# DIN recommendation layer: the loop over the history, laid out by four groups of 32 partitions

## The chip, the core and the metric

The kernel runs on one core of a Trainium2 chip. The metric is the device time of one execution in microseconds (us). The kernel before takes 36928.09 us, the median of 3 runs (36926.46 to 36942.14). A separate execution under the hardware profiler gives the profile; its own time was 36762.96 us, of which the program's span (first to last instruction) is 36760.7 us.

## The reference

A batch of 16384 users, each with a history of 200 items; all tables have rows of d = 64 float32 values. Cut to what matters:

```
h    = i_emb[hist]                                  # (200, 16384, 64): a gather
feat = concat([h, it, h - it, h * it])              # it: the candidate item, the same for all 200
a    = dice(feat @ au_W1 + au_b1, au_alpha, axis=1) # 36 hidden units; moments over the batch
w    = a @ au_W2 + au_b2                            # one weight for each (history place, user)
cur  = sum(w * h, axis=0)                           # (16384, 64)
z    = concat([u_emb[user], it, c_emb[cate], cur])
z    = dice(z @ W1 + b1, alpha1, axis=0); z = dice(z @ W2 + b2, alpha2, axis=0)
out  = z @ W3 + b3

dice(x, alpha): p = sigmoid((x - mean) / sqrt(var + 1e-8)); x * (p + alpha * (1 - p))
```

The moments of the first dice are those of one history place over the whole batch, so a place's gates can be worked out only when all 16384 users of that place have gone through the first layer.

## The kernel before

**The table.** Since `feat @ au_W1` is linear in `h` but for the product term, a first stage builds in DRAM a `table` with 128 values for each of the 100000 items: the row `h` (64 values) and `h @ (W_h + W_diff)` (36 values, padded). It also forms `xi`, the share of the candidate item with the bias, `itT`, the candidate rows turned, and `ucT`, the rows of user and category turned for the last layers. In this first stage each block of the table goes through `transpose` (L223), a matmul (L240) and `transpose_back` (L231).

**The loop.** The batch is cut into ND = 8 parts of 2048 users: TD = 16 tiles of 128 rows each. The loop runs over 200 places times 8 parts, so over 1600 steps, plus ten steps that only drain. A hardware loop (`For_i`) holds 24 places (192 steps) and runs 7 times; the last 32 places and the drain are written out. The order of the work on each engine is the order in the code (`manual_schedule`). One `step(k)` works on four parts at once:

- `fetch(k)`: 16 indirect DMAs from GpSimd (POOL, L202), each of 128 table rows of 512 bytes, into `land[k % 12]`, and one plain DMA of `xi` from SyncE (SP, L369) into `xit[k % 2]`.
- the gates of part k-10, on ScalarE (ACT): sigmoid of x (L452), then a scale and an offset per hidden unit (L455), into the PSUM tile `pg`.
- `turn(k-1)`: both halves of the gathered rows are turned so that d, or the hidden unit, lies on partitions. VectorE (DVE) transposes blocks of 32 x 32. Four instructions over 64 partitions each (L377), because a turned part has the 64 values of d on two groups of 32 partitions and two sets of rows beside them. ACT copies the turned rows into PSUM (`ph`, L458).
- `hidden(k-2)`: x = `px` + the turned table part (L390), written over the table half of `land`, and the batch statistics (L392).
- ACT copies `xit` into `px` (L462), and `product(k-1)`: `hm` = rows times candidate (L384), then `blk_m` times `hm` onto `px` on TensorE (PE, L240).
- `weights(k-10)`: gates times x (L398), a transposition back over 128 partitions (L400), a sum over 32 values (L402).
- `weigh(k-10)`: the two partial sums of a row lie on different partitions, so 64 partitions are moved (`r1`, L410) and added with the bias into PSUM (`w`, two instructions of 64 partitions, L413); then w times the rows (L418) and the sum onto `cur` (L419).
- every eighth step, `moments`: the statistics of two groups of partitions are joined by four copies of 32 partitions (L429) and a chain of small DVE instructions (L431 to L254), with a square root on ACT (L249).

`land` has 12 buffers, and step k-2 is the last to read the buffer that `fetch(k)` writes. Most DVE instructions of the loop take one operand from PSUM and one from SBUF. After the loop come two dense layers and the output.

Of the kernel before, what the change touches and what calls it, by code (L numbers as in the profile page):

```python
# [28 lines left out]
def din_kernel(  # L29
# [50 lines left out]

    parts = [(0, S), (S, A - S)]

# [3 lines left out]
    blk_h = once.tile([P, P], F32, name="blk_h")  # L86
    blk_i = once.tile([P, P], F32, name="blk_i")
    blk_m = const.tile([P, P], F32, name="blk_m")
    au_w = once.tile([P, 4, A], F32, name="au_w")
    au_bias = const.tile([P, 1], F32, name="au_bias")  # L90
    au_al = const.tile([P, 1], F32, name="au_al")
    au_1al = const.tile([P, 1], F32, name="au_1al")
    au_w2 = const.tile([P, 1], F32, name="au_w2")
# [4 lines left out]
    for e in range(2):  # L98
        rows = au_W1.rearrange("(g d) a -> d g a", d=D)[e * S : (e + 1) * S]
        for g in range(2):  # L100
            r = quarter(e, g)
            nc.sync.dma_start(au_w[r], rows)
            for q, (a0, n) in enumerate(parts):
                c, a = quarter(q, g, n), slice(a0, a0 + n)
                nc.vector.tensor_add(blk_h[r, c], au_w[r, 0, a], au_w[r, 2, a])
                nc.vector.tensor_sub(blk_i[r, c], au_w[r, 1, a], au_w[r, 2, a])
                nc.vector.tensor_copy(blk_m[r, c], au_w[r, 3, a])
    for g in range(2):
        for q, (a0, n) in enumerate(parts):
            r, a = quarter(q, g, n), slice(a0, a0 + n)  # L110
            nc.sync.dma_start(au_bias[r], col(au_b1)[a])
            nc.sync.dma_start(au_al[r], col(au_alpha)[a])
            nc.sync.dma_start(au_w2[r], au_W2[a])
# [11 lines left out]
    idx = [const.tile([P, NT], I32, name=f"idx{i}") for i in range(IDX)]  # L125
    stats = [const.tile([P, 2 * ND, nc.vector.BN_STATS_DIM], F32, name=f"st{i}") for i in range(2)]
    rstds = [const.tile([P, 1], F32, name=f"rs{i}") for i in range(2)]
    shifts = [const.tile([P, 1], F32, name=f"sh{i}") for i in range(2)]
    px, pz = (psum.tile([P, CD], F32, name=n) for n in ("px", "pz"))
# [6 lines left out]
    ucT = dram.tile([2, ND, P, CD], F32, name="ucT")  # L136
# [18 lines left out]
        n: const.tile([n * m, n * m], F32, name=f"mean{n}") for n, m in ((ZA, 2), (ZB, 2 * J), (Z2, 2))  # L155
# [53 lines left out]
    def load_ids(t, ids):  # L209
        nc.sync.dma_start(t, ids.rearrange("(p n) -> p n", n=NT))  # L210

# [3 lines left out]
    def by_tile(t, i):  # L215

        return t[:, ts(i, CH)].rearrange("p (n t) -> p n t", t=S)

    def transpose(dst, rows, n=TD):

        for i in range(2):
            for e in range(2):
                nc.vector.transpose(  # L223
                    by_tile(dst[ts(e, D)], i)[:, :n], rows[ts(i, D), :n, ts(e, S)]
                )

    def transpose_back(rows, src, n=TD):

        for i in range(2):
            for e in range(2):  # L230
                nc.vector.transpose(  # L231
                    rows[ts(i, D), :n, ts(e, S)], by_tile(src[ts(e, D)], i)[:, :n]
                )

    def layer(dst, pairs, n=CH, onto=False):

        for i in range(2):
            cols = slice(i * CH, i * CH + n)
            for j, (lhsT, rhs) in enumerate(pairs):
                nc.tensor.matmul(  # L240
                    dst[:, cols], lhsT, rhs[:, cols],
                    start=(j == 0 and not onto), stop=(j == len(pairs) - 1),
                    skip_group_check=onto,
                )
# [13 lines left out]
    ids = [once.tile([P, NT], I32, name=f"ids{i}") for i in range(3)]  # L258
    for t, v in zip(ids, (r_item, r_user, r_cate)):
        load_ids(t, v)  # L260
# [11 lines left out]
    def table_rows(b):  # L272
# [11 lines left out]
        transpose(rT, tab, m)  # L284
        layer((px, pz)[b % 2], [(blk_h, rT)], n=m * S)
        tabs[b] = tab, m

    def table_store(b):
        n0, n = blocks[b]
        tab, m = tabs.pop(b)  # L290
        transpose_back(tab[:, :, D:], (px, pz)[b % 2], m)
# [9 lines left out]
    def keep_one(j):  # L301
        c, k = j % ND, j // ND
        if k == 0:
            transpose(itT[:, c], land[j % EARLY])
            layer(ph, [(blk_i, itT[:, c])])
            t = pre.tile([P, CD], F32, tag="t", name="t")
            nc.scalar.activation(t, ph, AF.Identity, bias=au_bias)
            nc.scalar.dma_start(xi[c], t)
        else:
            t = pre.tile([P, CD], F32, tag="t", name="t")  # L310
            transpose(t, land[j % EARLY])
            nc.scalar.dma_start(ucT[k - 1, c], t)
# [22 lines left out]
    with ExitStack() as main:  # L335
# [15 lines left out]
        layer(px, [(blk_m, hx[0][:, 0])])  # L351
        nc.vector.bn_stats(stats[-1 % 2][:, 0, :], hx[0][:, 0, :CH])
        for c in range(1, 2 * ND):
            nc.vector.tensor_copy(stats[-1 % 2][:, c, :], stats[-1 % 2][:, 0, :])
# [16 lines left out]
        def turn(k):  # L371

            rows = land[k % LAND].rearrange("p n (s e c) -> p n s e c", s=2, e=2)
            for i in range(2):
                for e in range(2):
                    dst = hx[k % 2][ts(e, D), :, ts(i, CH)]
                    nc.vector.transpose(  # L377
# [293 lines left out]
```

## Time and profile before

| | |
|---|---|
| median of 3 runs | 36928.09 us |
| profiled execution | 36762.96 us |
| its span | 36760.7 us |
| POOL, first loop gather to last | 590.45 to 36527.96 us of the span |
| DVE busy | 25445.5 us (69%) |
| POOL busy | 24516.5 us (67%) |
| ACT busy | 7755.0 us (21%) |
| PE busy | 6368.2 us (17%), mean granted clock 0.542 |
| DMA | 73 GB/s on average |

In a row of the groups stand the line, the engine, the operation, what it writes and reads, the shapes and how often; then the busy time in us and the mean of one in ns; then the time for which the engine was idle just before such instructions, and what ended it. "issue" means that the engine waited for nothing that the profile shows.

### The profile page before, as it was taken

Reading aid. Unit: us, or ns where it says so; the run is one execution under the profiler, and the core shown is the slowest. Engines: PE = TensorE matmul, PEld = TensorE weight load, DVE = VectorE, ACT = ScalarE, POOL = GpSimd, SP = SyncE. Lnnn points to the kernel's source line nnn. Section 1 sums busy time; section 2 is a strip of 40 time slices with the busy share of each in tenths; the row PEclk is TensorE's granted clock in tenths of the full one; section 3 lists DMA queues with packets and bytes.
Section 4 is the critical chain, followed back from the end, with each engine's and each line's share of the span. In section 5 each row is a group of like instructions: output and inputs, shape, how many; then the busy total and the mean of one; then the engine's idle time right before and its main releaser. Section 6 shows DMA issues by size and latency. Waiting matters only on the chain. (4 is left out here: it accounts for less than half of the span.)

```text
span 36760.7 us, 100656 instructions
## 1 busy us (share of the span) xinstructions
PE 6368.2 (17%) x7006; PEld 2037.9 (6%) x7006; DVE 25445.5 (69%) x28797; ACT 7755.0 (21%) x7105; POOL 24516.5 (67%) x25991
## 2 busy tenths in 40 slices
PE   2111111111111111111111111111111111221112
PEld 0000000000000000000000000000000000000000
DVE  6767666676667666676667666676767666676767
ACT  0222222222222222222222222222222222222222
POOL 6666666666666666666666666666666666666665
PEclk5555555555555555555555555555555555555555
DMA  4222222222222222222222222222222222222222
GB/s 138 71 71 71 70 70 70 72 71 70 70 71 71 70 70 70 72 70 70 70 71 71 70 71 69 71 71 70 71 70 71 70 71 74 80 79 73 71 71 59
DMA packets 1214773, 2667.86 MB, mean 73 GB/s; under 512 B 551244, under 2 KB 577388, under 8 KB 1207916
## 3 DMA queue, kind: packets, MB, share of 16 engines
q0 software_dynamic: 831488, 1691.97, 17.5%
q1 hardware_dynamic: 372012, 906.09, 8.1%
q10 hardware_dynamic: 10560, 63.79, 0.4%
q14 instruction: 692, 5.67, 0.1%
q8 instruction: 21, 0.34, 0.0%
HBM read 2590.90 MB, written 69.16 MB: 72 GB/s over the span
## 5 line engine op out<-in xcount | busy, mean ns | idle before, releaser
L202 POOL DMA_INDIRECT land<-table,idx x25600 | 24153.1, 943 | 11825.8 <-issue 11629.5
L240 PE MATMUL px<-hx,blk_m 128*128 128x512 f32 x6408 | 5929.4, 1080 | 29931.8 <-DVE hx L384 15789.1
L377 DVE STREAM_TRANSPOSE hx<-land 64x1024 f32<-64x1024 f32 x6404 | 7920.8, 1237 | 2071.6 <-issue 1973.1
L452 ACT ACTIVATE pg<-land,sh,rs 128x1024 f32<-128x1024 f32 x1610 | 1943.8, 1207 | 18443.1 <-DVE cur L419 12618.3
L240 PEld LDWEIGHTS px<-hx,blk_m 128*128 128x128 f32 x6408 | 1880.8, 324 | 33947.3 <-issue 33947.3
L413 DVE SCALAR_TENSOR_TENSOR ph<-r,au_bias,r 64x16 f32<-64x16 f32 x3220 | 775.5, 241 | 3084.0 <-issue 2883.1
L458 ACT COPY ph<-hx 128x1024 f32<-128x1024 f32 x1601 | 1627.6, 1017 | 5996.1 <-DVE hx L377 3240.6
L418 DVE TENSOR_TENSOR pg<-land,ph 128x1024 f32<-128x1024 f32 x1610 | 1978.4, 1229 | 1190.7 <-issue 1158.6
L402 DVE TENSOR_REDUCE r<-hx 128x32 f32<-128x1024 f32 x1610 | 1964.1, 1220 | 584.2 <-issue 342.4
L400 DVE STREAM_TRANSPOSE hx<-pg 128x1024 f32<-128x1024 f32 x1610 | 2012.8, 1250 | 233.1 <-DVE pg L398 133.3
L392 DVE BATCH_NORM_STATS2 st<-land 128x6 f32<-128x512 f32 x3204 | 2061.2, 685 | 55.1
L390 DVE TENSOR_TENSOR land<-px,hx 128x1024 f32<-128x1024 f32 x1602 | 1962.1, 1225 | 69.7 <-issue 21.2
L419 DVE TENSOR_TENSOR cur<-pg,cur 128x1024 f32<-128x1024 f32 x1610 | 1970.9, 1224 | 55.6
L398 DVE TENSOR_TENSOR pg<-pg,land 128x1024 f32<-128x1024 f32 x1610 | 1957.3, 1216 | 2.7 <-ACT pg L455 2.5
L384 DVE TENSOR_TENSOR hx<-ph,itT 128x1024 f32<-128x1024 f32 x1601 | 1945.2, 1215 | 0.0
L455 ACT ACTIVATE pg<-pg,au_al,au_1al 128x1024 f32<-128x1024 f32 x1610 | 1895.0, 1177 | 54.4
L462 ACT COPY px<-xit 128x1024 f32<-128x1024 f32 x1601 | 1627.2, 1016 | 403.3 <-issue 257.6
L410 DVE COPY r<-r 64x32 f32<-64x32 f32 x1610 | 370.7, 230 | 1194.5 <-issue 976.6
L429 DVE COPY other<-mv 32x2 f32<-32x2 f32 x804 | 139.0, 173 | 1134.5 <-issue 1133.8
L249 ACT ACTIVATE std<-var,eps 128x1 f32<-128x1 f32 x201 | 59.2, 294 | 3361.8 <-DVE var L439 2823.8
L452 ACT ACT_TABLE_LOAD x209 | 268.1, 1283 | 394.1 <-DMA table<-tab 320.0
L439 DVE SCALAR_TENSOR_TENSOR var<-dev,half 128x1 f32<-128x1 f32 x201 | 44.2, 220 | 437.1 <-remote 411.2
(122 smaller groups left out, 2101.9 us busy)
## 6 DMA issues: line engine op xcount, KB each, us to landing
xit<-xi SPq DMA_DIRECT2D x1601, 512.0 KB
land<-table,idx POOLq DMA_INDIRECT x25600
table<-tab ACTq DMA_DIRECT2D x48, 1024.0 KB
tab<-in_L_rec_i_emb SPq DMA_DIRECT2D x48, 512.0 KB
zt<-ucT SPq DMA_DIRECT2D x32, 512.0 KB
idx<-in_r_hist SPq DMA_DIRECT2D x200, 64.0 KB
ucT<-t ACTq DMA_DIRECT2D x16, 512.0 KB
zbase<-zt SPq DMA_DIRECT2D x10, 512.0 KB
```

The source lines that it names most:

```text
L202: nc.gpsimd.indirect_dma_start(out=dst[:, n, :], out_offset=None, in_=rows, in_offset=bass.IndirectOffsetOnAxis(ap=ids[:, n : n + 1], axis=0),
L240: nc.tensor.matmul(dst[:, cols], lhsT, rhs[:, cols], start=(j == 0 and not onto), stop=(j == len(pairs) - 1), skip_group_check=onto,)
L377: nc.vector.transpose(dst.rearrange("p s (n t) -> p n s t", t=S), rows[ts(i, D), :, :, e])
L384: nc.vector.tensor_mul(hm, ph, itT[:, k % ND])
L390: nc.vector.tensor_add(x_of(k), by_row(px), by_row(hx[k % 2][:, 1]))
L392: nc.vector.bn_stats(stats[l % 2][:, 2 * c + i, :], x_of(k)[:, ts(i, TD // 2)])
L398: nc.vector.tensor_mul(by_row(pg), by_row(pg), x_of(k))
L400: nc.vector.transpose(yT, pg)
L402: nc.vector.tensor_reduce(r, yT.rearrange("p (i n u) -> p i n u", i=2, u=S), mybir.AxisListType.X, ALU.add)
L418: nc.vector.tensor_mul(by_row(pg), rows, w.unsqueeze(2).to_broadcast([P, TD, D]))
L419: nc.vector.tensor_add(cur[:, ts(c, TD)], by_row(pg), cur[:, ts(c, TD)])
L452: nc.scalar.activation(by_row(pg), x_of(k - 10), AF.Sigmoid, bias=shifts[i], scale=rstds[i])
```

## The change

A part is now laid out with the 128 rows of a tile on four groups of 32 partitions throughout. d (and the hidden unit) is split into two halves of 32, which lie side by side along the free axis and no longer on partitions. So each transposition covers 128 partitions in one instruction (two for `turn`, one of them straight into PSUM), `blk_h`, `blk_i` and `blk_m` become four matrices (which half of d goes in, which half of the units comes out), and the first layer contracts the two halves of d one after the other (`first_layer`, 4 matmuls where `layer` had 2). Biases, scales and moments become two columns, one for each half of the units, so the gates take four ACT instructions of half the size. The row sums of the weights now end on the partitions of their rows: the move and the two additions (L410, L413) are gone, and one `scalar_tensor_tensor` adds the bias and multiplies by the rows. Moments are averaged over the four groups by two small matmuls with `mean_of[S]`. `px` has two buffers in the hardware loop. ACT no longer copies into `ph`. For the last layers the old layout stays (`transpose_for_head`), so the candidate's rows are stored in DRAM too (`uicT`, 24 parts where `ucT` had 16).

```diff
+    def first_layer(dst, blk, rhs, n=CH, onto=False):
+        for q in range(2):
+            for e in range(2):
+                nc.tensor.matmul(
+                    dst[:, q * CH : q * CH + n], blk[:, e, q], rhs[:, e * CH : e * CH + n],
+                    start=(e == 0 and not onto), stop=(e == 1), skip_group_check=onto,
+                )
...
-        transpose(rT, tab, m)
-        layer((px, pz)[b % 2], [(blk_h, rT)], n=m * S)
+        nc.vector.transpose(halves(rT, m), of_rows(tab[:, :, :D], m))
+        first_layer(pxs[b % 2], blk_h, rT, n=m * S)
...
-        transpose_back(tab[:, :, D:], (px, pz)[b % 2], m)
+        nc.vector.transpose(of_rows(tab[:, :, D:], m), halves(pxs[b % 2], m))
...
         def turn(k):
-            rows = land[k % LAND].rearrange("p n (s e c) -> p n s e c", s=2, e=2)
-            for i in range(2):
-                for e in range(2):
-                    dst = hx[k % 2][ts(e, D), :, ts(i, CH)]
-                    nc.vector.transpose(
-                        dst.rearrange("p s (n t) -> p n s t", t=S), rows[ts(i, D), :, :, e]
-                    )
-        def product(k):
-            hm = hx[k % 2][:, 0]
+            rows = land[k % LAND]
+            hm, hw = hx[k % 2][:, 0], hx[k % 2][:, 1]
+            nc.vector.transpose(halves(ph), of_rows(rows[:, :, :D]))
             nc.vector.tensor_mul(hm, ph, itT[:, k % ND])
-            layer(px, [(blk_m, hm)], onto=True)
+            nc.vector.transpose(halves(hw), of_rows(rows[:, :, D:]))
...
+        def gates(k):
+            i = k // ND % 2
+            for q in range(2):
+                nc.scalar.activation(
+                    by_row(pg)[:, ts(q, TD // 2)], x_of(k)[:, ts(q, TD // 2)], AF.Sigmoid,
+                    bias=shifts[i][:, q : q + 1], scale=rstds[i][:, q : q + 1],
+                )
+            for q in range(2):
+                nc.scalar.activation(
+                    pg[:, ts(q, CH)], pg[:, ts(q, CH)], AF.Identity,
+                    bias=au_al[:, q : q + 1], scale=au_1al[:, q : q + 1],
+                )
...
-            r = small.tile([P, 2, TD], F32, tag="r", name="r")
+            r = small.tile([P, TD], F32, tag="r", name="r")
             nc.vector.tensor_reduce(
-                r, yT.rearrange("p (i n u) -> p i n u", i=2, u=S), mybir.AxisListType.X, ALU.add
+                r, halves(yT).rearrange("p q n u -> p n q u"), mybir.AxisListType.XY, ALU.add
             )
-            r1 = small.tile([D, 2, TD], F32, tag="r1", name="r1")
-            nc.vector.tensor_copy(r1, r[D:])
-            w = ph[:, :TD]
-            for i in range(2):
-                nc.vector.scalar_tensor_tensor(
-                    w[ts(i, D)], r[:D, i], au_bias2[:D], r1[:, i], ALU.add, ALU.add
-                )
-            nc.vector.tensor_mul(by_row(pg), rows, w.unsqueeze(2).to_broadcast([P, TD, D]))
+            nc.vector.scalar_tensor_tensor(
+                by_row(pg), r.unsqueeze(2).to_broadcast([P, TD, D]), au_bias2, rows,
+                ALU.add, ALU.mult,
+            )
             nc.vector.tensor_add(cur[:, ts(c, TD)], by_row(pg), cur[:, ts(c, TD)])
...
+        def moments_by_row(l):
+            mv = small.tile([P, 2, 2], F32, tag="mv", name="mv")
+            for q in range(2):
+                nc.vector.bn_aggr(mv[:, q], stats[l % 2][:, q].rearrange("p c s -> p (c s)"))
+            return mv
+        def mean_of_groups(mv):
+            nc.tensor.matmul(mean, mean_of[S], mv[:, :, 0], start=True, stop=True)
+        def var_of_groups(mv):
+            dev = small.tile([P, 2], F32, tag="dev", name="dev")
+            nc.vector.tensor_sub(dev, mv[:, :, 0], mean)
+            nc.vector.tensor_mul(dev, dev, dev)
+            nc.vector.tensor_add(dev, dev, mv[:, :, 1])
+            nc.tensor.matmul(var, mean_of[S], dev, start=True, stop=True)
+            std = small.tile([P, 2], F32, tag="std2", name="std2")
+            nc.scalar.activation(std, var, AF.Sqrt, bias=eps)
+            return std
+        def factors(l, std):
+            i = l % 2
+            nc.vector.reciprocal(rstds[i], std)
+            nc.vector.scalar_tensor_tensor(shifts[i], mean, -1.0, rstds[i], ALU.mult, ALU.mult)
...
         def step(k, last=None):
...
             if has(k - 10):
+                gates(k - 10)
+            if has(k - 2):
+                hidden(k - 2, px_of(k - 2))
+            if ends:
+                mv = moments_by_row(l)
+            if has(k - 1):
+                nc.scalar.copy(px_of(k - 1), xit[(k - 1) % XI])
+                turn(k - 1)
+            if ends:
+                mean_of_groups(mv)
+            if has(k - 10):
+                gated(k - 10)
+            if ends:
+                std = var_of_groups(mv)
+            if has(k - 1):
+                first_layer(px_of(k - 1), blk_m, hx[(k - 1) % 2][:, 0], onto=True)
+            if has(k - 10):
+                weigh(k - 10)
+            if ends:
+                factors(l, std)
```

## The prediction

> **What bounds the kernel now.** I read the stretches of the span first: before the loop, the wait for the table, the loop's gathers, the rest. The columns are the stretch, its length, then PE, PEld, DVE, ACT and POOL busy, each with its count.
>
> ```profile
> 0.00:549.00 549.00, 192.57 (x218) 55.88 (x218) 323.29 (x485) 10.19 (x9) 363.36 (x391) 0.60 0.58 171
> 549.00:590.00 41.00, 14.70 (x16) 4.50 (x16) 34.40 (x51) 0.35 (x1) 0.04 (x1) 0.54 0.58 201
> 590.00:36528.00 35938.00, 6046.26 (x6592) 1939.43 (x6592) 24903.50 (x28016) 7655.65 (x7014) 24153.12 (x25600) 0.54 0.26 71
> 36528.00:36761.00 233.00, 114.73 (x181) 38.10 (x180) 184.36 (x246) 88.85 (x82) 0.00 (x0) 0.66 0.07 24
> ```
>
> The loop is 35,938 of 36,761 us, 22.46 us for each of 1600 steps, and no engine is busy for over 70% of it. So the idle times matter. The costliest groups, by line:
>
> ```profile
> L202 POOL DMA_INDIRECT land<-table,idx x25600 | 24153.1, 943 | 11825.8 <-issue 11629.5
> L377 DVE STREAM_TRANSPOSE hx<-land 64x1024 f32<-64x1024 f32 x6404 | 7920.8, 1237 | 2071.6 <-issue 1973.1
> L400 DVE STREAM_TRANSPOSE hx<-pg 128x1024 f32<-128x1024 f32 x1610 | 2012.8, 1250 | 233.1 <-DVE pg L398 133.3
> L413 DVE SCALAR_TENSOR_TENSOR ph<-r,au_bias,r 64x16 f32<-64x16 f32 x3220 | 775.5, 241 | 3084.0 <-issue 2883.1
> ```
>
> POOL is the nearer to full. Its gathers take 0.943 us, and two that follow each other start 1.248 us apart (the idle 0.30 below comes before every gather). So 25,600 gathers cost at least 25,600 x 1.248 = 31,949 us; the other 35,938 - 31,949 = 3,989 us are pauses. The POOL timeline shows where they lie: at the end of a history place, where the moments hold up DVE, and shorter ones (2.0 to 3.4 us) in most other steps. Both end when DVE gives a `land` buffer back:
>
> ```profile
> 18280.87 0.94 POOL L202 DMA_INDIRECT land<-table,idx  x1 [14.48 <-issue]
> 18282.11 0.94 POOL L202 DMA_INDIRECT land<-table,idx  x1 [0.31 <-issue]
> ```
>
> So DVE sets the pace. Here is most of one DVE step of 22.4 us in the timeline (start, duration, idle before in brackets), then lines of one of 15.56 us:
>
> ```profile
> 18028.30 1.22 DVE L419 TENSOR_TENSOR cur<-pg,cur 128x1024 f32<-128x1024 f32 x1
> 18029.44 1.23 DVE L377 STREAM_TRANSPOSE hx<-land 64x1024 f32<-64x1024 f32 x1
> 18031.94 1.24 DVE L377 STREAM_TRANSPOSE hx<-land 64x1024 f32<-64x1024 f32 x1 [1.27 <-issue]
> ...
> 18044.54 0.18 DVE L410 COPY r<-r 64x32 f32<-64x32 f32 x1 [1.12 <-issue]
> 18045.94 0.23 DVE L413 SCALAR_TENSOR_TENSOR ph<-r,au_bias,r 64x16 f32<-64x16 f32 x1 [1.23 <-issue]
> 18048.05 0.24 DVE L413 SCALAR_TENSOR_TENSOR ph<-r,au_bias,r 64x16 f32<-64x16 f32 x1 [1.87 <-issue]
> 18049.44 1.23 DVE L418 TENSOR_TENSOR pg<-land,ph 128x1024 f32<-128x1024 f32 x1 [1.15 <-issue]
> ```
>
> ```profile
> 18296.87 4.99 DVE L377 STREAM_TRANSPOSE hx<-land 64x1024 f32<-64x1024 f32 x4
> ...
> 18309.48 0.58 DVE L413 SCALAR_TENSOR_TENSOR ph<-r,au_bias,r 64x16 f32<-64x16 f32 x2
> ```
>
> The work is the same, the 6.8 us between them are waits. They stand before the 64-partition instructions (L377 from the second on, L410, L413) and before L418 behind them; the 128-partition instructions in between (L390, L392, L398, L400, L384) follow each other without one. What ends these waits the profile doesn't show.
>
> **The change, part by part.**
>
> *DVE, one step.* I start from the 15.56 us without waits. Four L377 at 1.25 (4.99 together) become two transpositions over 128 partitions; L400 is the nearest row, 1.25, and 1.28 to the next start: -5.0 + 2.56. L410 and two L413 go: from L410's start (18309.26) to L418's (18310.10), -0.84. The new `scalar_tensor_tensor` replaces L418 (1.23); a small one takes 0.24 where a small tensor-tensor takes 0.16, so +0.08. L384, L390, L392, L398, L402, L419 stay. Sum: 15.56 - 5.0 + 2.56 - 0.84 + 0.08 = 12.4 us. Waits: below, none; above, each of the three forms without a row of its own (transposition into PSUM, transposition of the table half, the wide `scalar_tensor_tensor`) waits 1.9 as the worst L413 above, and L402 0.8 (it did so in some steps): 12.4 + 5.7 + 0.8 = 18.9 us. I take nearer the lower end, since L400, the same instruction over 128 partitions, waits 0.14 on average (233.1 us for 1610).
>
> *POOL, one step.* 16 x 1.248 = 19.97 us, unchanged. It is above both ends for DVE: POOL becomes the bound, and DVE's own saving past 20 us brings nothing. `fetch(k+1)` needs the end of step k-1. That step's `turn(k-2)` waits for gathers that land some 3 us after `fetch(k-1)` starts, and has about 10 us to go from there; `fetch(k+1)` starts 40 us after `fetch(k-1)`. So POOL has 27 us in hand.
>
> *PE.* Four records of 3.75 us a step become eight, 7.5 us. `hm` is followed on DVE by 1.28 (transposition) + 1.25 + 1.28 + 1.14 + 1.3 + 1.14 = 7.4 us before the next `hidden` asks for `px`; PE may hold DVE for up to 1 us. It lies under POOL's 20. *ACT.* 4.42 us a step lose L458 (1.02) and L452 and L455 (2.4) become four halves: 1.2 to 2.4 a pair, and 0.29 (the 128x1 root, L249) plus half of the rest makes 0.75 each, 3.0 in all, so 4.0 us; the gates run beside `hidden` and `turn` (6.2 us of DVE). Cost on the path: nothing; if POOL did not cover them, at most 1 us a step each. *DMA* of the loop is unchanged.
>
> *Moments, 200 times.* POOL paused 14.48 us there. Two `bn_aggr` (at most 0.58 each), five small DVE instructions (0.16 to 0.22), two PE visits (0.3 each), a root and its table load (0.29 + 1.28) come to some 5 us, and up to 13 us more if each of five small ones waits the 2.6 us that L439 waited at worst here. 18.9 + 18 = 37 us for such a step overshoots 20 by 17, less than the 27 in hand. Pause taken: nothing, 200 x 0 to 5.
>
> *Turns of the hardware loop, 7.* Before, POOL stood still for 24 us, since DVE had two steps to catch up; now DVE's last step ends before POOL's last gather, and about 3 to 4 us stay (DVE's last instruction ended at 17850.4, POOL began at 17853.3). 7 x 4 = 28; ends 20 to 60.
>
> *Before the loop.* POOL's 384 gathers took until 549.0 and the loop's first came at 590.4 after 41.4 us for the table. DVE's share: 49 blocks of eight instructions of 0.71 (278 us) become two of 1.25 (123 us). Unhindered, POOL needs 10 + 384 x 1.248 = 489; some table work is still behind it: 530, ends 505 and 590. The set-up (ten memsets; 16 `bn_stats` where one and 15 copies were) still makes the third `fetch` wait: 10.55 before, 15 now, ends 10 and 25.
>
> *After the last gather*: 233 us before, with two DVE steps of backlog (21 us from there to the last `turn`); now 3 us. 233 - 18 - some ten steps that are under 1 us shorter = 210, ends 190 and 233.
>
> **Sum** of the profiled execution: 530 + 15 + 31,949 + 28 + 210 + 2.3 (36,762.96 - 36,760.7) = 32,734 us. The median before is 165 us above its profiled execution; as I can't tell whether that offset stays, I add half: **32,820 us** (-11%). Ends: 505 + 10 + 31,949 + 20 + 190 + 2 = 32,676 without offset; 590 + 25 + 31,949 + 60 + 233 + 2 + 165 = 33,024 with it.
>
> **A rule against the change.** The row first: L413 reads `r` and `r1`, both from SBUF; at 18045.94 it ran inside a gather (18045.58, 0.94 us), and the next gather started 1.25 us after that one, so nothing was lost. The wide instruction that replaces L418 reads `r` and `land`, both from SBUF, where L418 took `w` from PSUM. The Trainium skill, "SBUF — State Buffer", section "Who interferes with whom", says that a VectorE instruction with two SBUF inputs contends with a GpSimd instruction that reads SBUF, and that the later one blocks for the whole instruction. By that rule POOL could lose one such instruction in each step and the sum would be up to 34,790; by the row it loses nothing and the sum stands.
>
> **The rivals.**
>
> 1. *The gathers are held by the wide `scalar_tensor_tensor`.* Price: L418's 1.23 us x 1600 = 1,968 us, so up to 34,790. Against: L413 and the small moments instructions never delayed a gather. For: none of them lasted over 0.3 us, too short to show. 0.08.
> 2. *DVE stays the bound because the new forms wait longer.* It decides from 19.97 us a step, 7.6 us of waits; at 21.2 us it makes 1.2 x 1600 = 1,970 more, at 22.4 us all of the steps' gain is gone and the moments alone are saved. 33,100 to 36,700. Against: only three forms are new, so 2.5 us each. 0.07.
> 3. *Slower: the waits belong to running beside gathers, not to 64 partitions.* Then all ten DVE instructions of a step wait 1.2 us each, as L377's second does: 12.4 + 12 = 24.4 us x 1600 = 39,040, and 39,800 with both ends of the program. It beats the time before from 10 us of waits a step. Against: L390 to L384 ran without waits beside gathers in the very step shown. 0.05.
>
> **How the numbers follow.** Forecast 0.80. What can be told from no change is about 0.2%, 74 us. The forecast and rivals 1 and 2 are faster: 0.94, after a hundredth for rival 2 ending within 0.2%; slower 0.05. The range goes from 32,600 (the low end, less some 75 for runs unlike the profiled one) to 33,800, which takes in the forecast's ends and half of rivals 1 and 2.
>
> **What would show it.** L202 still 943 ns, its idle time near 25,600 x 0.305 = 7,810 us with few pauses over 1 us; DVE waiting at `turn` for the gathers' DMA; DVE busy near 20,500 us (12.4 x 1600 and the rest of the program); transpositions at 1.25 us without "issue" idle. Wrong if POOL's pause at the moments stays, if gathers start over 1.25 us apart, or if the wide `scalar_tensor_tensor` or the transpositions show waits of over 2 us.

## The result: the change moved the wait, not the time

| | before | after |
|---|---|---|
| median of 19 runs each | 36937.4 us | 37010.46 us (36976.75 to 37058.87) |
| profiled execution, its span | 36762.96, 36760.7 us | 36985.32, 36983.5 us |
| first loop gather, last gather's end | 590.4, 36528.0 us | 606.1, 36781.7 us |
| DVE busy | 25445.5 us (69%) | 20049.6 us (54%) |
| POOL's pauses | 3.98 ms | 4.12 ms |

The ratio after to before is 1.002, with an interval of 1.0013 to 1.0027. The forecast of 32,820 us is missed by 4.2 ms, and the sign is wrong too: slower, by just about what can be told from no change (0.2%). (POOL's pauses, here and below, are worked out from the trace: of every two gathers that start over 1.4 us apart, the time over 1.248 us, summed.)

First the stretches of the span after, with the columns as before: length, then PE, PEld, DVE, ACT and POOL busy.

```profile
549.00:590.00 41.00, 14.85 (x25) 6.07 (x26) 15.57 (x17) 0.00 (x0) 11.33 (x12) 0.71 0.57 184
590.00:36528.00 35938.00, 9681.31 (x13721) 3868.76 (x13721) 19546.94 (x18908) 6948.61 (x8555) 24761.17 (x25424) 0.62 0.26 71
```

In the same stretch of 35,938 us VectorE now works 19.5 ms where it worked 24.9 ms: the 5.4 ms are really gone from its work. But the stretch holds 25,424 gathers, fewer than the 25,600 of before. The groups of the page say where the time went:

```profile
L212 POOL DMA_INDIRECT land<-table,idx x25600 | 24929.8, 974 | 11288.1 <-issue 11053.1
L396 DVE TENSOR_TENSOR land<-px,hx 128x1024 f32<-128x1024 f32 x1602 | 1959.1, 1223 | 15628.3 <-remote 13918.8
L389 DVE STREAM_TRANSPOSE ph<-land 128x1024 f32<-128x1024 f32 x1601 | 1992.7, 1245 | 478.4 <-DMA land<-table,idx 474.6
L427 DVE SCALAR_TENSOR_TENSOR pg<-r,au_bias,land 128x1024 f32<-128x1024 f32 x1610 | 2084.3, 1295 | 56.7
```

The transpositions and the wide `scalar_tensor_tensor` wait for next to nothing (478 and 57 us in the whole run). Nearly all the waiting stands before L396, `hidden`: 15,628 us, 9.8 us a step. The releaser is "remote" on the page; in the program that instruction stands behind a wait for TensorE's semaphore. (A semaphore is the counter with which an engine or a DMA tells that something is done; its rise is called a signal here.) POOL's idle time is still 11,288 us, 3.5 ms over the 25,600 x 0.305. VectorE's timeline of one step (start, duration, idle before):

```profile
18462.53 1.22 DVE L431 TENSOR_TENSOR cur<-pg,cur 128x1024 f32<-128x1024 f32 x1
18473.96 1.23 DVE L396 TENSOR_TENSOR land<-px,hx 128x1024 f32<-128x1024 f32 x1 [10.20 <-remote]
18475.22 1.29 DVE L398 BATCH_NORM_STATS2 st<-land 128x6 f32<-128x512 f32 x2
18476.42 1.24 DVE L389 STREAM_TRANSPOSE ph<-land 128x1024 f32<-128x1024 f32 x1
...
18485.10 1.22 DVE L431 TENSOR_TENSOR cur<-pg,cur 128x1024 f32<-128x1024 f32 x1
18496.42 1.23 DVE L396 TENSOR_TENSOR land<-px,hx 128x1024 f32<-128x1024 f32 x1 [10.10 <-remote]
```

and the product that the second L396 waits for, on PE's timeline, with the POOL gather that comes after VectorE has given a buffer back:

```profile
18479.07 6.61 PE L243 MATMUL px<-hx,blk_m 128*128 128x512 f32 x8 [16.62 <-DVE hx L390]
18485.80 0.94 POOL L212 DMA_INDIRECT land<-table,idx  x1 [2.60 <-issue]
```

The step is 22.46 us again (18473.96 to 18496.42). The eight records of the product end at 18485.68 (ends of matmul records are modelled), but the trace has TensorE's signal at 18496.32, 10.6 us later. Over the run the median from a product's first record to its signal is 17.3 us, for the 1,382 of 1,603 products whose signal has a record ahead of the next product; in the trace of before it is 3.77 us for four records, the time of the records themselves (1,045 of 1,602 products). Of the 1,369 waits of over 3 us before L396, 1,195 end within 0.2 us of a record of TensorE's signal. From the signal VectorE needs L396, L398, L389 and L390 until the next product can start, 5.1 us: 17.3 + 5.1 = 22.4. Because `hidden(k-2)` stands ahead of `turn(k-1)` in VectorE's order, the gathered rows lie unread meanwhile, and POOL waits for `land`.

So the first theory (A) was that VectorE's order behind TensorE's late signal costs it. Two rivals: B, something behind the gathers needs 1.40 us for each of them (16 x 1.40 = 22.4), whatever VectorE does, since both kernels take 22.4 to 22.6 us a step on average; C, the wide product with two SBUF inputs holds the gathers.

### The profile page after: what moved, and what is told of

It reads as the page before. It is cut to its first block, busy times and chain, and to the rows that moved or that the text cites. A ratio compares the mean times of both kernels' runs of the same rounds, so it can differ in the third digit from the quotient of the medians.

```text
span 36983.5 us, 116856 instructions
## 1 busy us (share of the span) xinstructions
PE 10134.8 (27%) x14456; PEld 4044.4 (11%) x14456; DVE 20049.6 (54%) x19476; ACT 7101.7 (19%) x8732; POOL 25299.4 (68%) x25992
## 5 line engine op out<-in xcount | busy, mean ns | idle before, releaser
L212 POOL DMA_INDIRECT land<-table,idx x25600 | 24929.8, 974 | 11288.1 <-issue 11053.1
L243 PE MATMUL px<-hx,blk_m 128*128 128x512 f32 x12824 | 9461.7, 906 | 22646.0 <-DVE hx L390 15979.1
L396 DVE TENSOR_TENSOR land<-px,hx 128x1024 f32<-128x1024 f32 x1602 | 1959.1, 1223 | 15628.3 <-remote 13918.8
L404 ACT ACTIVATE pg<-land,sh,rs 128x512 f32<-128x512 f32 x3220 | 2515.7, 781 | 23511.4 <-issue 21445.8
L243 PEld LDWEIGHTS px<-hx,blk_m 128*128 128x128 f32 x12824 | 3683.8, 302 | 28262.8 <-issue 27321.7
L409 ACT ACTIVATE pg<-pg,au_al,au_1al 128x512 f32<-128x512 f32 x3220 | 2419.0, 751 | 106.9
L389 DVE STREAM_TRANSPOSE ph<-land 128x1024 f32<-128x1024 f32 x1601 | 1992.7, 1245 | 478.4 <-DMA land<-table,idx 474.6
L427 DVE SCALAR_TENSOR_TENSOR pg<-r,au_bias,land 128x1024 f32<-128x1024 f32 x1610 | 2084.3, 1295 | 56.7
L398 DVE BATCH_NORM_STATS2 st<-land 128x6 f32<-128x512 f32 x3204 | 2061.2, 685 | 55.1
L422 DVE TENSOR_REDUCE r<-hx 128x16 f32<-128x1024 f32 x1610 | 1964.0, 1220 | 55.3
L390 DVE TENSOR_TENSOR hx<-ph,itT 128x1024 f32<-128x1024 f32 x1601 | 1959.5, 1224 | 54.7
L391 DVE STREAM_TRANSPOSE hx<-land 128x1024 f32<-128x1024 f32 x1601 | 1974.6, 1233 | 0.0
L243 PE MATMUL px<-rT,blk_h 128*128 128x512 f32 (+1 forms) x392 | 236.1, 764 | 237.6 <-DVE rT L294 124.7
```

Source lines behind the costliest of these rows:

```text
L212: nc.gpsimd.indirect_dma_start(out=dst[:, n, :], out_offset=None, in_=rows, in_offset=bass.IndirectOffsetOnAxis(ap=ids[:, n : n + 1], axis=0),
L243: nc.tensor.matmul(dst[:, q * CH : q * CH + n], blk[:, e, q], rhs[:, e * CH : e * CH + n], start=(e == 0 and not onto), stop=(e == 1), ski ...
L389: nc.vector.transpose(halves(ph), of_rows(rows[:, :, :D]))
L390: nc.vector.tensor_mul(hm, ph, itT[:, k % ND])
L391: nc.vector.transpose(halves(hw), of_rows(rows[:, :, D:]))
L398: nc.vector.bn_stats(stats[l % 2][:, q, c, :], x_of(k)[:, ts(q, TD // 2)])
```

## The experiments

Of 18 runs, the first four were on one chip and the others, in groups, on five more. The kernel before, which ran beside them every time, turned out to be the most telling of all. A diff is against the changed kernel unless another is named.

| run | before on that chip, us | this, us | POOL's pauses, ms | mean gather, ns |
|---|---|---|---|---|
| e1 hidden late | 36767.89 | 36818.45 | 3.83 | 989 |
| e2 r in PSUM | 36767.89 | 36808.6 | 3.89 | 964 |
| e3 both | 36767.89 | 36724.92 | 3.77 | 968 |
| e4 12 of 16 gathers | 36767.89 | 28770.0 | 3.92 | 987 |
| e6 gathers alone | 32735.53 | 32723.37 | 0.08 | 944 |
| e7 no product | 32735.53 | 32887.18 | 0.17 | 950 |
| e8 small DMAs | 32735.53 | 32927.71 | 0.28 | 951 |
| e9 half rows | 32735.53 | 33855.02 | 1.13, held gathers included | 987 |
| g1 the changed kernel | 32733.22 | 32794.9 | 0.14 | 946 |
| g2 the kernel before | 32733.22 | 32734.47 | 0.07 | 943 |
| i2 r in PSUM | 32734.5 | 32724.07 | 0.08 | 944 |

**e1: `hidden` and the moments behind the transpositions, the product and the gates' product.**

```diff
-            if has(k - 2):
-                hidden(k - 2, px_of(k - 2))
...
+            if has(k - 2):
+                hidden(k - 2, px_of(k - 2))
             if has(k - 10):
                 weigh(k - 10)
```

> In the loop, hidden(k-2) and the moments step stand behind turn, first_layer and gated of step k-1 instead of ahead of them; nothing else differs from the changed kernel. Theory A (VectorE's in-order queue): in most steps TensorE's semaphore for the moments-and-blocks product reaches VectorE about 17.4 us after the product's first matmul, and because hidden(k-2) waits for it ahead of the two transposes, the gathered rows stay unread and land's buffers run out; 17.4 + 1.26 + 1.2 + 1.28 + 1.22 = 22.4 us, the step that the trace shows. With hidden late the transposes and the wide product run while TensorE's signal is outstanding, the ring of 22.4 us is cut, and POOL sets the step: 16 x (974 + 305 ns) = 20.5 us, 25,600 x 1.279 = 32.7 ms and some 0.9 ms around and in the turns: 33.4 to 33.9 ms. Theory B (a server behind the gathers needs about 1.40 us for each row block, whatever VectorE does; 16 x 1.40 = 22.4 us): no change, 36.9 ms. Theory C (the wide product with two inputs in SBUF holds the gathers, and that sets the pace): no change, 36.9 ms.

Measured: 36818.45 us, 1.0014 of before (1.0005 to 1.0024). The ring that theory A names was cut, and in all nothing was won. The wait before L396 fell by a third and POOL's median step from 22.45 to 20.97 us, but the pause at the moments grew (table under e4), and the mean step is 22.48 us:

```profile
L396 DVE TENSOR_TENSOR land<-px,hx 128x1024 f32<-128x1024 f32 x1602 | 1954.3, 1220 | 10270.6 <-remote 7976.8
```

Theory A as a cause is refuted: TensorE's signal came later with respect to its product. The waits of over 1 us before L396 now end a median of 32.4 us after the first record of the product that it reads, where it was 17.3 us.

**e2: `r` in PSUM**, and **e3: both edits.**

```diff
-            r = small.tile([P, TD], F32, tag="r", name="r")
+            r = ph[:, 32 : 32 + TD]
```

> The transposed unit vectors' product r is taken as a slice of PSUM's tile ph instead of a tile in SBUF, so the wide scalar_tensor_tensor reads one input from SBUF and one from PSUM. Theory A (VectorE's queue behind TensorE's late signal): the gathers that overlap that instruction come down from a mean of 1186 ns to about 943 ns, POOL's busy time falls by up to 780 us, and the time stays within 0.5% of 36.98 ms, since POOL pauses for land's buffers anyway. Theory C (the held gathers set the pace): 36.2 ms or less. Theory B (1.40 us per row block behind the gathers): no change.

> Both edits: hidden and the moments step behind turn, first_layer and gated, and r in PSUM. Theory A: POOL sets the step at 16 x 1.248 = 20.0 us: 606 + 31,950 + 200 and some 60 in the loop's turns, 32.8 to 32.9 ms. Theory B: 36.9 ms. Theory C: no more than 36.2 ms, and the same as with r in PSUM alone.

Measured: e2 1.0012 of before (1.0003 to 1.0022), e3 0.9989 (0.9979 to 0.9998). Theory C falls with e2. In e3 the waits have moved on once more, to the instruction that overwrites `ph` behind the moments' matmuls:

```profile
L396 DVE TENSOR_TENSOR land<-px,hx 128x1024 f32<-128x1024 f32 x1602 | 1955.4, 1221 | 9828.4 <-remote 8092.8
...
L422 DVE TENSOR_REDUCE ph<-hx 128x16 f32<-128x1024 f32 x1610 | 1977.0, 1228 | 3698.0 <-remote 3349.2
```

**e4: 12 of the 16 gathers of each step** (a quarter of the rows is left out).

```diff
-            gather(land[k % LAND], idx[l % IDX][:, ts(c, TD)], table)
+            gather(land[k % LAND], idx[l % IDX][:, c * TD : c * TD + 12], table)
```

> Each step gathers 12 of its 16 row blocks (a quarter of the rows is left out); VectorE's and TensorE's instructions are those of the changed kernel. Theory A with a signal whose lateness does not depend on the number of gathers: the step stays at 22.4 us, 36 to 37 ms. Theory A with a lateness that shrinks as POOL idles more: between 12.4 us a step (VectorE's busy time, 20 ms in all) and 22 us. Theory B: 12 x 1.40 = 16.8 us a step, about 28 ms.

Measured: 28770.0 us, nearest to B's 28 ms, but not it. From the first to the end of the last gather it is 27,956 us, 17.5 us a step, where the changed kernel takes 22.6: four gathers less are worth 5.1 us, 1.28 us each, which is about POOL's own 1.25. What stays is the sum of the pauses: 3.92 ms, 2.4 us a step, as with 16 gathers. Where they lie moves. By the eight steps of a history place, in the hardware loop without its turns, POOL pauses (us):

| | before | after | e1 | e2 | e3 | e4 |
|---|---|---|---|---|---|---|
| the step held up by the moments | 10.7 | 7.1 | 10.4 | 6.1 | 12.9 | 14.0 |
| the seven others together | 8.6 | 12.6 | 7.9 | 12.7 | 5.0 | 5.0 |

Most of e4's steps took 15 to 16 us and the others much longer; their mean of 17.5 is not 12 x 1.40 = 16.8, so B's 1.40 us for each gather and nothing else is the wrong form of it. (Gathers 1.39 to 1.42 us apart do occur: 885 in after, 1,473 in e2, 126 in e4, none in before.) In the traces of before, of after and of e1 to e4, 2.4 to 2.6 us a step were lost, whatever the order, the operands or the number of gathers. Two numbers of gathers can't tell a loss per step beside POOL's own pace from something shared that needs 1.28 us for a gather and some 2 us for the rest of a step's signals; e8 was made for that, but met a chip of the other kind.

**e6 to e9**: the gathers alone, no product, more signals, half the bytes.

```diff
# e6, in step(k), behind fetch(k):
+            if last is None:
+                return
# e7:
-            if has(k - 1):
+            if last is not None and has(k - 1):
                 first_layer(px_of(k - 1), blk_m, hx[(k - 1) % 2][:, 0], onto=True)
# e8, in fetch(k):
+            for t in extra:
+                nc.sync.dma_start(t, xi[c][:16, :16])
# e9, in fetch(k):
-            gather(land[k % LAND], idx[l % IDX][:, ts(c, TD)], table)
+            gather(land[k % LAND][:, :, :D], idx[l % IDX][:, ts(c, TD)], i_emb)
```

> In the loop a step issues its 16 gathers and the two loads of ids and of the unit vectors' base, and nothing else (all of VectorE's, TensorE's and ScalarE's work of the loop's steps is left out). Theory B1 (the gathers themselves cannot be kept up faster than one in 1.40 us, whoever reads them): 25,600 x 1.40 = 35.84 ms and some 0.9 ms, 36.7 ms. Theory D (POOL keeps its 1.248 us as long as nothing makes it pause; the 2.4 us a step are lost to waits for the other engines): 25,600 x 1.248 = 31.95 ms and 0.9 ms, 32.9 ms, without pauses.

> TensorE's product is left out of the loop's steps (the unit vectors keep the base alone); VectorE's instructions, their order and the moments stay. Theory A (the late signal of TensorE's product is what VectorE's queue loses): hidden(k-2) waits for ScalarE's copy alone, no 17 us, and POOL sets the step at 16 x (974 + 305 ns) = 20.5 us: 33.4 to 33.9 ms. Theory B (1.40 us for each gather behind POOL): still 22.4 us a step, 36.7 to 37.0 ms, with the wait moved to another instruction.

> Four more transfers of 1 KB each (16 partitions, so that 16 DMA engines signal) are issued by SP in each step; nobody waits for them. If the server behind the gathers works off the signals of the DMA engines (16 for a gather, 22.4 us for the 17 transfers of a step, 1.32 us for each), four more make it 27.7 us a step, 45 ms. If it is bytes or rows that it works off, or if there is none: no change, 37.0 ms.

> The gathers take rows of 256 bytes from the embedding table itself in place of 512 bytes from the doubled one (the second half of each row is left out); number of gathers, rows and signals as before. If the 1.40 us are set by bytes, the step falls to POOL's 16 x 1.248 to 16 x 1.28 us: 32.9 to 33.7 ms. If they are set by the rows or by the signals, or if the step is VectorE's chain behind TensorE: no change, 36.7 to 37.0 ms.

They answer another question than the one put to them: on their chip the kernel before took 32735.53 us, 4.0 ms less than beside the first four runs, and e8, which is the changed kernel with something added, 32927.71 us. The condition that all these expectations were about was not there. What can be read: with the gathers alone in the hardware loop's 1344 steps (the last 256 keep all their work) the program needs 32723.37 us, which is POOL's pace without a pause,

```profile
L212 POOL DMA_INDIRECT land<-table,idx x25600 | 24166.8, 944 | 7864.0 <-issue 7679.1
```

(944 + 305 ns each), so before ran at POOL's floor there. 6,400 more transfers cost at most 0.2 ms, not 8. e9 is slower, since its gathers took 987 ns and its step mostly 21.0 us; it says nothing on the 36.8 ms, but much on the rule against the change (below).

**g1 to g4: the changed kernel, the one before, the gathers alone and the one without the product, unchanged, on one more chip.** 

> The changed kernel itself, once more, because the kernel before took 36.77 ms on one chip and 32.74 ms on another. Theory E (what costs 1.40 us for each gather is a condition of the chip and not of the kernel; where it is absent POOL's own 1.248 us set the pace of both): on a chip where before takes 32.7 ms, this takes 32.8 to 32.9 ms, TensorE's signal comes with the end of the product, and POOL's pauses come to some 0.3 ms; on a chip where before takes 36.8 ms, this takes 36.9 to 37.0 ms with TensorE's signal 11 us behind the product's end and 4 ms of pauses. Theory A alone (the new order of VectorE's work, whatever the chip): 37.0 ms everywhere.

> The kernel before itself, for its trace on this chip. Theory E: where it takes 32.7 ms, VectorE's waits ahead of the short instructions on 64 partitions are gone and a step takes 20.0 us throughout, so that the change has nothing to remove; where it takes 36.8 ms, steps of 22.4 us with these waits, as in the trace shown.

> The gathers alone, as before (all other work of the loop's steps left out). On a chip where the kernel before takes 36.8 ms this tells whether the gathers themselves cannot go faster than one in 1.40 us there (36.7 ms), or go at 1.248 us until another engine's signal is needed (32.7 ms). On a chip where it takes 32.7 ms: 32.7 ms again.

> The changed kernel without TensorE's product in the loop's steps (left out; moments kept). On a chip where before takes 36.8 ms: Theory A with the chip's late signal gives 33.4 to 33.9 ms, since no late signal is waited for; Theory B (1.40 us for each gather behind POOL, whoever waits) gives 36.7 to 37.0 ms. On a chip where it takes 32.7 ms: 32.9 ms again.

Measured: before 32733.22, after 32794.9, ratio 1.0019 (1.0009 to 1.0028); the gathers alone 32729.26, without the product 32800.01 us. Theory E's first half held: 32.79 ms where 32.8 to 32.9 was expected, with 0.14 ms of pauses where 0.3 was. The groups of before here show that its waits were no property of its instructions alone:

```profile
L377 DVE STREAM_TRANSPOSE hx<-land 64x1024 f32<-64x1024 f32 x6404 | 7937.8, 1240 | 6367.7 <-DMA land<-table,idx 6225.8 <-PEq L505 70.5 <-issue 7.0
L418 DVE TENSOR_TENSOR pg<-land,ph 128x1024 f32<-128x1024 f32 x1610 | 1977.4, 1228 | 54.9
L413 DVE SCALAR_TENSOR_TENSOR ph<-r,au_bias,r 64x16 f32<-64x16 f32 x3220 | 770.8, 239 | 114.8
```

L413 waited 3,084 us in the trace that the prediction was made from, and 115 us here; L418 1,191 and 55; the "issue" part of L377 1,973 and 7. L377 now waits for the gathers' DMA instead, as a consumer does whose producer is the bound. The changed kernel on the same chip:

```profile
L212 POOL DMA_INDIRECT land<-table,idx x25600 | 24224.9, 946 | 7877.7 <-issue 7129.8 <-DMA land<-table,idx 544.2 <-DVE st L398 140.5
L389 DVE STREAM_TRANSPOSE ph<-land 128x1024 f32<-128x1024 f32 x1601 | 2016.9, 1260 | 11655.3 <-DMA land<-table,idx 11655.3
L396 DVE TENSOR_TENSOR land<-px,hx 128x1024 f32<-128x1024 f32 x1602 | 1947.5, 1216 | 353.3 <-PE px L243 237.1 <-PEq L530 105.2 <-issue 11.1
```

and a stretch of its timelines, the wait for the gathers and the product, whose signal comes a median of 5.92 us after its first record:

```profile
18475.13 1.26 DVE L389 STREAM_TRANSPOSE ph<-land 128x1024 f32<-128x1024 f32 x1 [7.62 <-DMA land<-table,idx]
```

```profile
18477.79 5.25 PE L243 MATMUL px<-hx,blk_m 128*128 128x512 f32 x8 [13.28 <-DVE hx L390]
```

This is the picture that the prediction drew: VectorE waits 7.3 us a step at `turn` for the DMA, and POOL sets the pace. Only, before sits at the same floor.

**h1 to h3: each kernel with 8 of 16 gathers, so that POOL needs 10 us a step and VectorE shows** (half of the rows left out; the gathers alone once more beside them). The edit is that of e4 with 8 for 12, in the changed kernel and in the one before.

> The gathers alone (all other work of the loop's steps left out). On a chip where the kernel before takes 36.8 to 36.9 ms: 36.7 ms if the gathers cannot be kept up faster than one in 1.40 us there; 32.7 ms if POOL keeps its 1.248 us and the loss comes only when another engine's signal is waited for. On a chip where before takes 32.7 ms: 32.7 ms.

> The changed kernel with 8 of a step's 16 gathers (half of the rows left out), so that POOL needs 10.0 us a step. If VectorE's work is what the prediction summed, 12.4 us a step and some 4 us more at each of the 200 moments: 1,600 x 12.4 + 0.8 ms + 0.8 ms, 21.2 to 21.8 ms. If something takes 1.40 us for each gather (11.2 us a step) it lies under that. If TensorE's late signal comes with any gather traffic: 22.4 us a step, 36 ms.

> The kernel before with 8 of 16 gathers. Its quick steps in the trace took 15.56 us, VectorE's work without the waits: 1,600 x 15.5 and 0.9 ms, 25.5 to 26.0 ms; so the change takes some 4 ms of VectorE's time out of the loop, all of it hidden while POOL needs 20 us a step. If VectorE's waits of the slow steps come with any gather traffic: 22.4 us a step, 36 ms.

Measured, with 32733.97 us for before in full and 32733.46 us for the gathers alone: 20877.19 us after, 26213.69 us before. The busy times of the engines, first after, then before:

```profile
PE 10147.1 (49%) x14456; PEld 4046.9 (19%) x14456; DVE 19927.8 (95%) x19478; ACT 7086.3 (34%) x8732; POOL 12482.1 (60%) x13192
```

```profile
PE 6359.1 (24%) x7006; PEld 2042.6 (8%) x7006; DVE 25342.0 (97%) x28799; ACT 7755.9 (30%) x7105; POOL 12436.5 (47%) x13191
```

Both are bound by VectorE, and the change is worth 5,336 us there, 3.3 us a step. After ended 0.3 ms below its expected range and before 0.2 ms above its own.

**i1, i2: what the 62 us are** that the changed kernel takes more at POOL's floor: the gathers alone, and `r` in PSUM (the edit of e2), on one more chip.

> The gathers alone (all other work of the loop's steps left out). On a chip where the kernel before takes 36.8 to 36.9 ms: 36.7 ms if the gathers cannot be kept up faster than one in 1.40 us there; 32.7 ms if POOL keeps its 1.248 us and the loss comes only when another engine's signal is waited for. On a chip where before takes 32.7 ms: 32.7 ms.

> The changed kernel with r in PSUM, so that the wide product has one input in SBUF. Where before takes 32.73 ms and the changed kernel 32.79 ms: if its 60 us are gathers that the wide product lengthens (a mean of 946 in place of 943 ns over 25,600 gathers is 72 us), POOL's mean comes back to 943 ns and the time to 32.73 to 32.75 ms; if they are the moments' pauses (some 70 us more than before), it stays at 32.79 ms. Where before takes 36.8 to 36.9 ms: as measured there already, within 0.3% of before.

Measured: the gathers alone 32739.17 us; i2 32724.07 us, 0.9997 of before (0.9987 to 1.0006).

```profile
L212 POOL DMA_INDIRECT land<-table,idx x25600 | 24153.6, 944 | 7877.2 <-issue 7205.6
```

Of g1's gathers, 3,191 overlap the wide instruction and take 966 ns on average, the others 943; with `r` in PSUM the two kinds take 944 and 943. The 71 us of POOL's busy time are back, and the time with them. It is the best version, level with before and with the gathers alone; no version with these 25,600 gathers can beat POOL's floor.

**j1: four quarters of 48 steps in each turn of the loop**: full steps, 8 of 16 gathers, no product, the gathers alone (the edits above, by quarter; 48 of the steps behind the loop have 8 gathers too).

> Each turn of the loop (192 steps) has four quarters of 48 steps: the changed kernel's full steps; the same with 8 of 16 gathers; full gathers without TensorE's product; gathers alone (so parts of the rows and of the work are left out, as named). On a chip where before takes 32.7 ms: 20.0, 12.4, 20.0 and 20.0 us a step, 30.0 ms. On a chip where before takes 36.8 to 36.9 ms, Theory B1 (1.40 us for each gather whoever waits): 22.4, 12.4 to 14, 22.4 and 22.4 us a step, about 32.9 ms; Theory D (POOL keeps its own pace until a late signal is waited for): 22.4, 12.4 to 14, 20 to 22 and 20.0 us a step, about 31.3 to 32 ms.

Measured: 29800.55 us, beside 32746.21 us for before. By the starts of the gathers the quarters take 20.01, 12.3, 20.04 and 20.08 us a step (second turn; the others within 0.35). This chip, too, was of the 32.7 ms kind, so what the run was for stays open.

## Why the prediction was wrong, point by point

**The step that failed, in the result's runs: PE.** The text said "PE may hold DVE for up to 1 us. It lies under POOL's 20." PE held VectorE for 10.2 us a step, and the sum of it and VectorE's chain is 22.4 us, over POOL's 20. The 7.5 us for eight records was near (6.6 us here, by the modelled ends); missing was that the signal can reach the waiting engine 10.6 us after the modelled end of the last record, which no row of before showed for TensorE (L390 waited 69.7 us in the whole run). e1 shows that the other order tried does not help.

**The premise behind it: who owned the waits.** The text said of them "What ends these waits the profile doesn't show", and then priced the change as if they belonged to the 64-partition instructions they stood before. On a chip of the other kind the same instructions wait for next to nothing (g2), and on the first two occasions the loss came back in whatever form the kernel offered: at L377 and L413 in before, at L396 in after, at L396 and L422 in e3. The 3,989 us of pauses that the text found were the quantity to hold on to: 4.12, 3.83, 3.89, 3.77 and 3.92 ms in five other kernels. In before they are not TensorE's: of VectorE's 9.7 ms of idle time between 700 and 32,400 us, 6.5 ms stand before instructions that wait for VectorE's own signals alone (L413 among them) and 2.9 ms before instructions that wait for no semaphore (the second L377 of most steps among them); in g2 it is 0.5 and 0.1 ms. A rival "the pauses stay, whoever waits" would have given 36.7 to 36.9 ms; none of the three rivals was that one. Rival 2 allowed up to 36,700, but for waits at three new forms, which waited 0.3 us a step together; rival 3 had all ten instructions wait, and nine did not.

**VectorE's step, 12.4 us: right.** 12.3 us in j1's second quarter, moments included, and 12.6 over all of h2's gathers; the difference of the two kernels is 3.3 us a step by h2 and h3, where the sum said 15.56 - 12.4 = 3.2.

**POOL as the bound, 19.97 us a step: right on five chips, wrong on the result's.** There the sum for the profiled execution, 32,734 us, stands against 32796.54 (g1), and the forecast of 32,820 against a median of 32794.9. By its terms: before the loop 530, measured 489, below the lower end of 505 (606 in the result); the third `fetch` 15, measured 13.4 beyond the usual 1.25; the gathers 31,949, measured 25,600 x 1.2485 = 31,962; turns of the loop 28, measured some 62 (six starts 8 to 12 us apart and one 4, less the usual 1.25), and six some 29 us apart in the result; after the last gather 210, measured 204 (202 in the result); other pauses, which were taken as nothing, 65. The half of 165 us that was added for the median has no counterpart: g1's median lies 2 us below its profiled execution. Some of these misses cancel, so that 32,820 came within 25 us of g1 is in part luck. And the same floor holds for before, so the saving that was forecast, 11%, existed on neither kind.

**Moments, "pause taken: nothing": wrong in the result's runs**, where the step that they hold up pauses POOL by 7 us on average; 0.2 us in g1.

**The rule against the change: right, but it strikes few gathers.** The row was silent for a reason: its gather had started 0.36 us before L413, and a gather that already runs is not held. In the ten runs that have the wide `scalar_tensor_tensor` with `r` in SBUF in the loop all 5,326 gathers that start 0.10 to 1.10 us after it end some 0.81 us after its end, whenever they started; of the 4,889 that start in its first 0.09 us at most a thousandth takes over 0.96 us. Two lines of e9, start and duration:

```profile
15009.99 1.29 DVE L427 SCALAR_TENSOR_TENSOR pg<-r,au_bias,land 128x1024 f32<-128x1024 f32 x1
15010.14 1.95 POOL L212 DMA_INDIRECT land<-in_L_rec_i_emb,idx  x1 [0.30 <-issue]
```

The Trainium skill, "SBUF — State Buffer", section "Who interferes with whom", says that a VectorE instruction with two SBUF inputs contends with a GpSimd instruction that reads SBUF and that the order of issue decides which of them is blocked; that a whole instruction is lost it says in so many words of VectorE's 2-port modes only. The traces agree for the gather: when it comes second it waits, up to 1.06 us, and one operand in PSUM ends it (i2). L413, which came second to a gather, took its usual 0.23 us, so the other direction is not seen there. What it costs hangs on when the two meet. In g1 the gathers keep time with VectorE's steps, and of the 3,191 that overlap the wide instruction only 324 take over 0.96 us: 71 us in all, not the 1,968 that were priced. In e9, 1,282 are held, 977 of them to over 1.9 us: 1,069 us, which is what e9 takes over g1 on another chip (33855.02 and 32794.9 us). In the result's trace the gathers that overlap it take 1186 ns, and there it did not matter (e2).

**What stays open:** in what the two kinds of chips differ, and so what makes the pauses. The gathers alone on a chip of the 36.8 ms kind were not seen, since no later run landed on one. It is not the speed of the instructions: L377 takes 1237 ns in the result's trace of before and 1240 in g2, and the granted clock is 0.54 and 0.55. Nor do the gathers' data come late: the last of a gather's 16 packets of 4 bytes ends a median of 2.2 us after its start in before and after, 2.1 us in g1 and g2, and their packets of 4096 bytes take a median of 220 ns in before and after, 211 in e3, g1 and g2. Even the first gather of the loop comes some 100 us later (590 to 606 us against 489).

One difference is in every trace: the records of signals. In g2 there are 20,980 of them for the 20,978 signals that VectorE's instructions raise and 448,391 for the 448,432 of the DMAs; in before it is 10,390 and 53,071, though the packets of 4 bytes, 16 to a gather, are all there. After and e1 to e4 are like before, the other runs like g2. That is why so many waits end with "issue" or "remote" in such a trace. Whether signals are merged there or only their records lost, and whether it is the cause of the pauses or another result of what causes them, no run tells. Of the signals that do have a record, ScalarE's come with the end of their instruction in before and after, TensorE's in before too but mostly not in after. It is not the profiler that costs the time: without it before takes 165 us more. Whether all this belongs to the chip or to the hour can't be told either: each occasion had one chip, and before stayed within 0.1% on it.

## What to carry to other kernels

An idle time that the profile ends with "issue" or "remote" need not belong to the instruction it stands before: hold on to the total loss of the bounding engine, give a real chance to the case that this total stays, and only then price the edit. Run the unchanged kernel on a second chip before explaining a loss with no visible releaser; here that one number, 32.73 for 36.94 ms, would have ended the argument. When an engine's own floor explains a loop's time to 0.3% (25,600 gathers of 1.248 us, 31,949 of 32,025 us in g2), work taken off another engine is worth nothing until there are fewer gathers; with half of them the same change was worth 5.3 ms. And when the total of the pauses stays while an edit moves them from one step to another, as in e1, e3 and e4, the edit has not reached their cause.

## What the runs showed of the hardware that was not expected

- The same kernel takes 36.75 to 36.95 ms on some occasions and 32.73 to 32.75 ms on others, stable within each, with most gathers 1.25 us apart in both. The 4 ms are POOL's pauses, 2.4 to 2.6 us a step in six traces of six kernels.
- In those six traces 10 to 14% of the DMAs' signals and about half of VectorE's (39 to 50%) have a record; in the others over 99% have one.
- TensorE's signal can come 10.6 us after the modelled end of its last matmul (a median of 17.3 us after the first record) while gathers run, and with the end of it on another chip (5.9 us).
- In e3 those signals mostly come 22.40 or 21.70 us apart (483 and 222 of 1,745 distances), and others at 5.60, 7.70, 42.70 and 44.80 us, all multiples of 0.70 us; what has that beat is not known.
- A gather that starts 0.10 to 1.10 us after a 128x1024 `scalar_tensor_tensor` with two SBUF inputs (1.3 us) ends some 0.81 us after that instruction (all 5,326 of them); one that starts ahead of it or in its first 0.09 us takes its usual 0.94 us.
